# A decoder layer on one core: the self-attention output in seven block products, with new places for the mask and the first loads

## The chip, the cores and the metric

The kernel runs on one core of a Trainium2 chip. A core has five instruction queues that matter here: TensorE (PE, with PEld for its weight loads), VectorE (DVE), ScalarE (ACT), GpSimd (POOL) and SyncE (SP, which only issues transfers). Sixteen DMA engines move the data. The metric is device microseconds of the whole program, less is better. A measured time is the median of several runs; a profile is one further execution, with its own time.

## The reference, cut to what matters

The layer takes x of shape 8 x 256 x 1024 (eight batches, 256 tokens, 1024 features) and computes, all in float32:

```python
x = layernorm(x + self_attention(x))          # 32 heads of 32, 8 key/value heads, rotary, causal
x = layernorm(x + cross_attention(x, ctx))    # 32 heads of 128, 8 key/value heads, rotary, mask
x = layernorm(x + memory_ffn(x))

def self_attention(h):
    ...
    out = attn @ v                            # per head, put together to [8, 256, 1024]
    return out @ wo.T                         # wo 1024 x 1024
```

The change is about the last line, `out @ wo.T`, and about when some inputs are loaded. Per batch it is a product of 256 x 1024 by 1024 x 1024.

## The kernel before

Batches are counted from 0. Self-attention runs in 64 steps: step s belongs to batch b = s // 8 and to chunk c = s % 8, which is a group of four heads (128 features). The loop over s is at L508. It projects queries two steps ahead (`query(s + 2)`), makes scores one step ahead, and sums values for two steps at once: the even step of a pair only makes scores, the odd one does `weighted` in two halves. Between these the step does one thing from `others(s)` (L400). For c below 4 and b above 0 that is a quarter of the output projection of the batch before: `project_out(b - 1, c)` (L361) makes 128 tokens by 512 features in eight matmuls and adds it to the residual tile with one VectorE operation (L372). The quarters c = 0, 1 use the left half of the output weight, c = 2, 3 the right half. When both halves of a token tile are done, `moments` (L126 to L132) starts its norm; the reciprocal root is a GpSimd operation (L132). In chunks 4 to 7 `others` makes keys and values of the next batch, and `turn` (L383) transposes the normed tiles for cross-attention and stores them (x1T).

The output weight is loaded again for each batch. `load_out(b, 0)` issues four transfers of 512 KB at the end of chunk 6, `load_out(b, 1)` four more at the end of chunk 1 of the next batch (L353 to L358, tile `sa_wo`, four buffers). SP issues in program order, so a load that must wait for a buffer holds all loads behind it. Other weights go through nine buffers `w4` (L109).

From step 4 to 59 the same steps also make the keys and values of cross-attention, already by a seven-product scheme: `products` is a list of parts, four per step, taken by `one()` at fixed places. What these parts make is turned and stored by GpSimd: rotary adds `kx` (L725) with a store, and value stores (L835). The scheme needs sums of weight blocks. GpSimd makes them in "events" (`sum_event`, L483): event e issues the loads of its own tile `ws` (two buffers) and then does the four sums of event e - 1 (L417) and stores them to memory (L440, L466). As there are two buffers, the loads of event e wait until the stores of event e - 2, which were issued in event e - 1, have landed. The list `steps` says in which steps the events fall; one of a step's events comes right after `others`, the rest at the step's end (L567).

TensorE, GpSimd and SP run in exactly the order in which the program is written. VectorE and ScalarE are ordered by a planner.

The prologue (L493 to L506) loads the key weights of batch 0 and all of its input, makes both key projections, two queries, the scores of step 0 and the values of batch 0, and then loads the stored values back in a turned layout (`load_values`), which SP must wait for.

The passage to cross-attention starts at the end of step 61 with `xa_early`, which loads the first normed input (x1T), tables, keys, and last the mask; `mask_bias` turns the mask to a bias after the loop. In the wait listings SPq stands for SP's queue.

Of the kernel before, what the change touches and what calls it, by code (L numbers as in the profile page):

```python
# [8 lines left out]
F32 = mybir.dt.float32  # L9
# [3 lines left out]
ALU = mybir.AluOpType  # L13
# [7 lines left out]
P = 128  # L21
B, S, E = 8, 256, 1024
# [49 lines left out]
class Layer:  # L72
# [74 lines left out]
    def self_attention(self):  # L147
# [12 lines left out]
        def load_x(b):  # L160
            xTs[b] = ep.tile([P, KC, S], F32, name="xT", bufs=2)
            nc.sync.dma_start(out=xTs[b], in_=a["xT"][b])
# [10 lines left out]
        def load_kv(b, name):  # L173

            for i in range(2):
                src = a[name][:, :, i * P : (i + 1) * P] if name == "sa_wk" else a[name][:, 4 * i : 4 * i + 4, :]
                wkvs[b, name, i] = self.weights([P, *src.shape[1:]], src)

        load_kv(0, "sa_wk")
        load_x(0)  # L180
        nc.scalar.dma_start(out=rot, in_=a["sa_rot"])
        nc.scalar.dma_start(out=sin, in_=a["sa_sin"])
        nc.scalar.dma_start(out=cos, in_=a["sa_cos"])
# [1 line left out]
        def signed():  # L185

            ones = sp.tile([P, 1], F32, name="sa_ones")
            nc.gpsimd.memset(ones, 1.0)
            ps = self.mm()
            nc.tensor.matmul(ps[:, 0:1], lhsT=rot, rhs=ones, start=True, stop=True)  # L190
            sign = sp.tile([P, 1], F32, name="sign")
            nc.vector.tensor_copy(sign, ps[:, 0:1])
            nc.vector.tensor_scalar(sin, sin, sign, None, ALU.mult)
# [26 lines left out]
            nc.vector.tensor_tensor(turned, turned, sin, ALU.mult)  # L220
            nc.vector.tensor_tensor(dst, turned, dst, ALU.add)

        kTs, vs, v_d, qTs, ats, oTs = {}, {}, {}, {}, {}, {}

        def keys(b, i):
            if i == 0:
# [3 lines left out]
            rope(kTs[b][:, i, :], project(wkvs.pop((b, "sa_wk", i)), xTs[b]))  # L230

        def values(b, tt):
            if b and tt == 0:
                load_kv(b, "sa_wv")
            ps = self.mm()
            for k in range(KC):
                nc.tensor.matmul(
                    ps[:, :256], lhsT=xTs[b][:, k, tt * P : (tt + 1) * P],
                    rhs=wkvs[b, "sa_wv", k // 4][:, k % 4, :],
                    start=(k == 0), stop=(k == KC - 1),  # L240
                )
            rows = sp.tile([P, SA_KV * SA_D], F32, name="sa_vrow", bufs=2)
            nc.scalar.copy(rows, ps[:, :256])
            if tt == 0:
                v_d[b] = self.dram.tile([S, SA_KV * SA_D], F32, name=f"sa_v_{b}")
            nc.scalar.dma_start(out=v_d[b][tt * P : (tt + 1) * P, :], in_=rows)
# [69 lines left out]
        def weighted(s, rest):  # L316

            b, c = divmod(s, KC)
            at, v = ats[s // 2], vs[b, c // 4]
            if not rest:
                pos[s] = [p_sc.tile([P, 2, 512], F32, name="sc") for _ in range(2)]
            banks = [pos[s][i // 2][:, i % 2, :P] for i in range(4)]
            for k in range(3, BLOCKS) if rest else range(3):
                for i in range(max(k - 4, 0), 4):
                    rows = slice(32 * i, 32 * i + 32)
                    for j in range(4):
                        lo, block = (0, slice(2 * k, 2 * k + 2)) if k <= i else (  # L330
                            64, slice(2 * k + 1, 2 * k + 2) if k < 4 else slice(k + 4, k + 5)
                        )
                        nc.tensor.matmul(
                            banks[i][32 * j : 32 * j + 32, lo:], lhsT=v[rows, k, 32 * j : 32 * j + 32],
                            rhs=at[rows, j, block].rearrange("p x u q -> p (x u q)"),
                            start=(k == 0), stop=(k == 4 + i),
                        )
            if not rest:
                return
            del ats[s // 2], pos[s]  # L340
            oT = sp.tile([P, 2, S], F32, name="sa_oT", bufs=6)
            for i in range(4):
                nc.scalar.copy(
                    oT.rearrange("p u (t i q) -> p i t u q", t=2, i=4)[:, i],
                    banks[i].rearrange("p (t u q) -> p t u q", t=2, u=2),
                )
            for u in range(2):
                oTs[s - 1 + u] = oT[:, u, :]

        wos = {}  # L350
        norms = []

        def load_out(b, half):  # L353
            cols = slice(half * 512, (half + 1) * 512)
            wos[b, half] = []
            for c in range(0, KC, 2):
                w = sp.tile([P, 2, 512], F32, name="sa_wo", bufs=4)
                nc.sync.dma_start(out=w, in_=a["sa_wo"][:, c : c + 2, cols])  # L358
                wos[b, half].append(w)

        def project_out(b, i):  # L361
            half, tt = divmod(i, 2)
            t = 2 * b + tt
            cols = slice(half * 512, (half + 1) * 512)
            ps = self.mm()
            for c in range(KC):
                nc.tensor.matmul(  # L367
                    ps, lhsT=oTs[b * KC + c][:, tt * P : (tt + 1) * P], rhs=wos[b, half][c // 2][:, c % 2, :],
                    start=(c == 0), stop=(c == KC - 1),
                )  # L370
            x = self.res[t]
            nc.vector.tensor_tensor(x[:, cols], ps, x[:, cols], ALU.add)  # L372
            if half == 1:
                mv, rstd = self.moments(x, EPS)

                def norm():
                    nc.vector.tensor_scalar(x, x, mv[:, 0:1], rstd, ALU.subtract, ALU.mult)
                    self.x1[t] = self.dram.tile([P, E], F32, name=f"x1_{t}")
                    nc.scalar.dma_start(out=self.x1[t], in_=x)

                norms.append(norm)

        def turn(b, tt):  # L383

# [15 lines left out]
        def others(s):  # L400


            b, c = divmod(s, KC)
            parts = []
            if b and c < 4:
                parts.append(lambda: project_out(b - 1, c))
            elif c < 4 or 1 < b + 1 < B:
                parts.append([
                    lambda: values(b + 1, 0), lambda: values(b + 1, 1),
                    lambda: keys(b + 1, 0), lambda: keys(b + 1, 1),  # L410
                ][c % 4])
            if b and c in (5, 6):
                parts.append(lambda: turn(b - 1, c - 5))
            return parts
# [30 lines left out]
        def sums_of_outputs(g, u, half):  # L445
# [13 lines left out]
            def run():  # L459
# [6 lines left out]
                    nc.gpsimd.dma_start(out=self.wsums["xa_wo", g][i][:, u, cols], in_=t)  # L466
            return run


        sums = [lambda n=n, m=m, i=i: sums_of_inputs(n, m, i)  # L470
                for m in range(XA_KV // 2) for n in ("xa_wk", "xa_wv") for i in range(2)]
        sums += [lambda m=m, i=i: sums_of_inputs("xa_wq", m, i) for m in range(QP) for i in range(2)]
        sums += [lambda g=g, u=u, i=i: sums_of_outputs(g, u, i)
                 for g in range(XA_KV) for u in range(2) for i in range(2)]

        n = XA_KV * 2
        steps = [1 + e * 7 // 8 for e in range(n)]
        steps += [15 + e * (KV_END - 17) // (len(sums) - n) for e in range(len(sums) - n + 1)]  # L480
        made = []

# [7 lines left out]
        self.hp, self.raws = ep, 3  # L490
        products = [part for q in range(NQ) for m in range(XA_KV // 2) for part in self.xa_keys_values(q, m)]

        signed()  # L493
        keys(0, 0)
        load_query(0)
        load_kv(0, "sa_wv")
        keys(0, 1)
        load_query(1)
        load_x(1)
        load_query(2)  # L500
        query(0)
        values(0, 0)
        query(1)
        scores(0)
        values(0, 1)
        load_values(0, 0)  # L506
        last = SA_STEPS
        for s in range(last):  # L508
            b, c = divmod(s, KC)
# [44 lines left out]
            if s % 2:  # L554
                weighted(s, True)
                one()
                if s + 1 < last:
                    scores(s + 1)
            if c == 1:
                load_values(b, 1)  # L560
            elif c == 6:
                load_out(b, 0)
# [5 lines left out]
                event()  # L568
            if c == 7 and b + 1 < B:
                load_values(b + 1, 0)  # L570
            if b and c == 1:
                load_out(b - 1, 1)
            if b and c == 0 and b + 1 < B:
                load_x(b + 1)
            if first:
# [4 lines left out]
            if s == last - 3:  # L580
                early.close()
                self.xa_early()
                more = self.xa_query(1)
            if s == last - 1:
                psum.close()
                self.xa_psum()
        self.mask_bias()
# [17 lines left out]
    def xa_early(self):  # L605

        self.xp = self.hp = self.pool("xa_early", 1, side="right")
        self.raws = 2
        self.xb, self.kT, self.v, self.ats = {}, {}, {}, {}
        self.qT, self.atts, self.oT, self.wo, self.acc = {}, {}, {}, {}, {}  # L610
        self.queries = self.xa_query(0, eager=True)

        self.first_qTs = [self.qT_tile() for _ in range(2)]
        self.first_att = self.att_tile()
        self.bias = self.xp.tile([P, NB * 2, S], F32, name="bias")
        self.load_x1T(0)
        self.load_tables(0)
        self.load_keys(0)
        self.load_mask(0)

    def xa_psum(self):
        self.p_sc = self.pool("xa_sc", 2, space=PSUM)
# [973 lines left out]
```

## Time and profile before

| what | value |
|---|---|
| median of three runs | 3482.47 us (3478.1 to 3483.72) |
| the profiled execution | 3482.07 us |
| its span, first to last instruction | 3480.3 us |
| mean granted TensorE clock | 0.985 |
| busy PE / DVE / ACT / POOL | 97% / 61% / 35% / 30% |
| output projection of self-attention, TensorE (L367) | 224.8 us in 512 records |
| its adds, VectorE (L372) | 21.9 us, 32 of 686 ns |
| moved by DMA | 626.36 MB, mean 180 GB/s |

A line of the groups reads: line, engine, operation, out <- in, sizes, count, then busy us and mean ns of one, then idle us just before and what ended it. A line of a timeline reads: start, length, engine, line, operation, count, and in brackets the idle time before it with what ended it. A line of the waits reads: who waited for whom, us in total, times, longest us. "Releasers" are inferred from semaphores.

### The profile page before, as it was taken

How to read it: one execution, taken by the hardware profiler on the slowest of the kernel's cores; microseconds unless marked ns; L12 is line 12 of the kernel's file. 1: busy time of each engine (PE TensorE's matmuls, PEld its weight loads, DVE VectorE, ACT ScalarE, POOL GpSimd, SP SyncE). 2: the span in 40 equal slices, each digit the busy share in tenths (PEclk: the TensorE clock that was granted, in tenths of full speed). 3: DMA queues.
4: the chain of work that ended last, by engine and by line, in shares of the span. 5: the costliest groups of instructions: out<-in, count | busy, mean ns of one | idle time of the engine just before them, and what ended most of it. 6: DMA issues, size and time to landing. Idle time of an engine off the chain costs nothing.

```text
span 3480.3 us, 71081 instructions
## 1 busy us (share of the span) xinstructions
PE 3377.2 (97%) x27811; PEld 2448.8 (70%) x27811; DVE 2113.9 (61%) x6003; ACT 1202.3 (35%) x4030; POOL 1047.8 (30%) x1363
## 2 busy tenths in 40 slices
PE   7999999999999799999999999999999999999996
PEld 6777778787777567777667667676767766776763
DVE  4655565565566455665675566666665667566556
ACT  3434433343344333232223333223332333333224
POOL 3454655666655221121131112112111212121112
PEclk9999999999999899999999999999999999999998
DMA  7778788787877464444544444544444544444442
GB/s 234 231 245 271 262 267 266 264 279 246 285 270 240 167 192 150 136 138 132 167 149 146 125 127 137 163 143 149 135 131 131 161 146 146 133 127 135 130 148 97
DMA packets 269551, 626.36 MB, mean 180 GB/s; under 512 B 28961, under 2 KB 99761, under 8 KB 268193
## 3 DMA queue, kind: packets, MB, share of 16 engines
q1 hardware_dynamic: 194672, 441.00, 39.4%
q0 software_dynamic: 50032, 154.66, 14.0%
q10 hardware_dynamic: 24512, 26.15, 2.2%
q8 instruction: 221, 3.62, 0.4%
q14 instruction: 114, 0.93, 0.1%
HBM read 526.93 MB, written 94.77 MB: 179 GB/s over the span
## 4 chain that ended last, share of the span: by engine, by line
PE 61%; DVE 5%; POOL 1%; ACT 1%; issue 1%; DMA 1%; SPq 0%; POOLq 0%; DVEq 0%; ACTq 0%
PE mm L748 21%; PE mm L954 19%; PE mm L901 7%; PE sc L850 6%; PE mm L1232 2%; PE mm L367 2%; PE mm L1009 1%; PE mm L208 1%; PE mm L742 1%; POOL acc L983 1%; DVE res L983 0%; DVE t L723 0%; PE mm L1249 0%; DVE ln_st L126 0%; DVE xat L884 0%
## 5 line engine op out<-in xcount | busy, mean ns | idle before, releaser
L748 PE MATMUL mm<-x1T,w 128*128 128x256 f32 x3584 | 853.5, 382 | 15.3 <-DMA w<-xa_wq_sums 11.8
L748 PEld LDWEIGHTS mm<-x1T,w 128*128 128x128 f32 x3584 | 677.7, 191 | 201.6 <-issue 96.5
L954 PE MATMUL mm<-w,xoS 128*128 128x512 f32 x992 | 449.5, 596 | 0.0
L864 ACT ACTIVATE xatt<-xatt,nmax 128x256 f32<-128x256 f32 x512 | 257.2, 503 | 508.4 <-DVE nmax L859 499.0
L667 POOL DMA_DIRECT2D v<-v x256 | 151.4, 598 | 734.9 <-PE mm L901 616.9
L954 PE MATMUL mm<-w,xoT 128*128 128x512 f32 x744 | 338.1, 596 | 5.4 <-ACT xoT L909 4.1
L954 PEld LDWEIGHTS mm<-w,xoS 128*128 128x128 f32 x992 | 185.1, 190 | 193.3 <-issue 171.0
L208 PE MATMUL mm<-xT,w 128*128 128x256 f32 x1280 | 305.0, 395 | 9.3 <-DMA xT<-in_xT 9.3
L754 DVE TENSOR_TENSOR half<-mm,half 128x256 f32<-128x256 f32 x288 | 119.8, 416 | 291.7 <-PE mm L748 273.8
L208 PEld LDWEIGHTS mm<-xT,w 128*128 128x128 f32 x1280 | 246.4, 197 | 60.3 <-issue 25.0
L901 PEld LDWEIGHTS mm<-xat,v 32*128 32x128 f32 x8192 | 243.9, 187 | 53.4 <-issue 29.3
L920 POOL TENSOR_TENSOR xoS<-xoT 128x512 f32<-128x512 f32 x62 | 79.0, 1275 | 671.2 <-ACT xoT L909 670.9
L901 PE MATMUL mm<-xat,v 32*128 32x128 f32 x8192 | 269.9, 277 | 5.5 <-DVE acc L961 4.4
L289 ACT ACTIVATE att<-att,nmax 128x128 f32<-128x128 f32 (+1 forms) x512 | 225.5, 441 | 125.1 <-DVE nmax L284 124.9
L850 PE MATMUL sc<-kT,qT 128*128 128x256 f32 x1024 | 262.7, 380 | 0.0
L870 ACT ACTIVATE xatt<-xatt,rec 128x256 f32<-128x256 f32 x512 | 231.2, 499 | 88.1 <-DVE rec L868 87.7
L909 ACT COPY xoT<-mm 128x128 f32<-128x128 f32 x512 | 98.0, 275 | 470.0 <-PE mm L901 439.0
L754 DVE TENSOR_TENSOR raw<-mm,half 128x256 f32<-128x256 f32 x384 | 159.3, 415 | 159.2 <-PE mm L748 118.5
L417 POOL TENSOR_TENSOR ws<-ws 128x256 f32<-128x256 f32 x320 | 243.5, 761 | 27.8 <-DMA ws<-in_xa_wk 7.3
L954 PEld LDWEIGHTS mm<-w,xoT 128*128 128x128 f32 x744 | 138.7, 190 | 148.1 <-issue 127.3
L884 DVE STREAM_TRANSPOSE xat<-xatt 128x512 f32<-128x512 f32 x256 | 180.9, 707 | 74.7 <-ACT xatt L870 71.9
L367 PE MATMUL mm<-sa_wo,sa_oT 128*128 128x512 f32 x512 | 224.8, 592 | 0.0
(230 smaller groups left out, 4875.7 us busy)
## 6 DMA issues: line engine op xcount, KB each, us to landing
w<-xa_wq_sums SPq DMA_DIRECT2D x128, 512.0 KB, 3.7
w<-xa_wo_sums SPq DMA_DIRECT2D x124, 512.0 KB, 3.6
w<-in_xa_wo SPq DMA_DIRECT2D x97, 512.0 KB, 4.2
w<-in_sa_wq SPq DMA_DIRECT2D x64, 512.0 KB, 8.9
sa_wo<-in_sa_wo SPq DMA_DIRECT2D x64, 512.0 KB, 6.6
w<-in_xa_wq SPq DMA_DIRECT2D x64, 512.0 KB, 3.6
v<-v POOLq DMA_DIRECT2D x256, 128.0 KB
w<-xa_wk_sums SPq DMA_DIRECT2D x32, 512.0 KB, 8.6
```

Of the source, the lines that this page charges most:

```text
L208: nc.tensor.matmul(ps[:, :S], lhsT=lhs[:, k, :], rhs=xT[:, k, :], start=(k == 0), stop=(k == KC - 1),)
L289: nc.scalar.activation(att[:, jj, lo:hi], att[:, jj, lo:hi], AF.Exp, bias=nmax[:, i : i + 1], scale=-1.0, accum_out=sums[:, i : i + 1],)
L367: nc.tensor.matmul(ps, lhsT=oTs[b * KC + c][:, tt * P : (tt + 1) * P], rhs=wos[b, half][c // 2][:, c % 2, :], start=(c == 0), stop=(c == K ...
L417: nc.gpsimd.tensor_tensor(out, in0, in1, op)
L748: nc.tensor.matmul(ps[:, :S], lhsT=w[:, k, :], rhs=rhs[:, k, :], start=(k == 0), stop=(k == 3))
L754: nc.vector.tensor_tensor(out, in0, in1, ALU.add)
L850: nc.tensor.matmul(sc[:, qt, :], lhsT=qT[:, q0 : q0 + P], rhs=kT[:, b * S : (b + 1) * S], start=True, stop=True,)
L864: nc.scalar.activation(att[:, qt, :], att[:, qt, :], AF.Exp, bias=nmax[:, qt : qt + 1], scale=-1.0, accum_out=sums[:, qt : qt + 1],)
L870: nc.scalar.activation(att[:, qt, :], att[:, qt, :], AF.Identity, bias=0.0, scale=rec[:, qt : qt + 1])
L884: self.nc.vector.transpose(self.ats[M, b][:, :, u].rearrange("p c t j -> p t c j"), self.atts[H][b].rearrange("p t (c j) -> p t c j", j=32),)
L901: nc.tensor.matmul(banks[i][:, :P], lhsT=v[rows, c, :], rhs=at[rows, c, :], start=(c == 0), stop=(c == BLOCKS - 1),)
L954: nc.tensor.matmul(ps, lhsT=oT[lhs][:, u, off + p * P : off + (p + 1) * P], rhs=w[:, u, :], start=(u == 0), stop=(u == 1),)
```

## The change

For batches 1 to 6 the output projection is made by seven block products. The attention output of a batch, 256 x 1024, is split into 2 x 2 blocks of 128 x 512 (A11 to A22), the weight into 2 x 2 blocks of 512 x 512. Four sums of A blocks (S1 to S4) and four of weight blocks (T1 to T4) make seven products of four matmuls take the place of eight (four quarters of eight matmuls). Each product is added to up to four blocks of the residual: 14 additions per batch in place of 4. Chunk 0 makes P1 and P2, chunk 1 P6 and P5, chunk 2 P3 and P4, chunk 3 P7.

The sums of A are made by GpSimd: S1 and S2 at the end of chunk 7, S4 and S3 at the end of chunk 1, in each case behind the step's events. The sums of the weight are made once, by eight further events among the first, and stored; each is loaded again per batch. Each of the seven products loads its own 1 MB of weights (two transfers), at the ends of chunks 6, 0, 1 and 2.

In the prologue the first key weight and the first input are loaded in halves by turns, queries and scores of step 0 come before the values, the value weights of batch 1 are loaded there, and the values are loaded back in steps 0 and 1. The mask is loaded at the end of step 63.

```diff
-        load_kv(0, "sa_wk")
-        load_x(0)
+        for k in range(0, KC, 4):
+            nc.sync.dma_start(out=first_k[:, k : k + 4, :], in_=a["sa_wk"][:, k : k + 4, :P])
+            nc.sync.dma_start(out=xTs[0][:, k : k + 4, :], in_=a["xT"][0][:, k : k + 4, :])
...
         def load_out(b, half):
+            if 0 < b < B - 1:
+                return load_seven(b, ("P1", "P2")) if half == 0 else None
...
+        PARTS = {
+            "P1": ("A11", (0, 0)), "P2": ("A12", (1, 0)), "P3": ("S4", (1, 1)), "P4": ("A22", "T4"),
+            "P5": ("S1", "T1"), "P6": ("S2", "T2"), "P7": ("S3", "T3"),
+        }
...
+        def sum_heads(b, name):
+            out = sp.tile([P, 4, P], F32, name="sa_S", bufs=2)
+            pieces = [out[:, 0:2, :], out[:, 2:4, :]]
...
+            for o, u, v in zip(pieces, x, y):
+                nc.gpsimd.tensor_tensor(o, u, v, op)
...
+        def seventh(b, n):
+            ps = self.mm()
...
+            for k in range(4):
+                nc.tensor.matmul(
+                    ps, lhsT=left[k // 2][:, k % 2, :], rhs=w[k // 2][:, k % 2, :],
+                    start=(k == 0), stop=(k == 3),
+                )
+            return ps
...
+        def out_by_seven(b, c):
+            if c == 0:
+                add_to(b, seventh(b, "P1"), (0, 0), (0, 1), (1, 0), (1, 1))
+                add_to(b, seventh(b, "P2"), (0, 0))
+            elif c == 1:
+                add_to(b, seventh(b, "P6"), (0, 1), (1, 0), (1, 1))
+                add_to(b, seventh(b, "P5"), (0, 1), (1, 1))
+            elif c == 2:
+                add_to(b, seventh(b, "P3"), (0, 1))
+                norm_later(2 * b)
+                add_to(b, seventh(b, "P4"), (1, 0))
+            else:
+                add_to(b, seventh(b, "P7"), (1, 0), (1, 1))
+                norm_later(2 * b + 1)
...
+        for e in range(8):
+            sums.insert(3 * e + 2, lambda e=e: sums_of_sa(e // 2, e % 2))
...
-        n = XA_KV * 2
-        steps = [1 + e * 7 // 8 for e in range(n)]
+        n = XA_KV * 2 + 8
+        steps = [1 + (e - e // 3) * 7 // 8 for e in range(n)]
...
+        load_query(0)
+        load_query(1)
+        load_kv(0, "sa_wv")
+        nc.sync.dma_start(out=wkvs[0, "sa_wk", 1], in_=a["sa_wk"][:, :, P:])
+        load_query(2)
+        load_x(1)
         signed()
         keys(0, 0)
...
+        load_kv(1, "sa_wv")
+        query(0)
+        scores(0)
+        query(1)
+        values(0, 0)
+        values(0, 1)
+        keys(0, 1)
...
+            if s < 2:
+                load_values(0, s)
+            elif c == 1:
                 load_values(b, 1)
...
             while events:
                 event()
...
+            if c == 7 and 0 < b < B - 1:
+                sum_heads(b, "S1")
+                sum_heads(b, "S2")
+            if c == 0 and 0 < b - 1 < B - 1:
+                load_seven(b - 1, ("P6", "P5"))
+            if c == 2 and 0 < b - 1 < B - 1:
+                load_seven(b - 1, ("P7",))
             if b and c == 1:
                 load_out(b - 1, 1)
+                if 0 < b - 1 < B - 1:
+                    load_seven(b - 1, ("P3", "P4"))
+                    sum_heads(b - 1, "S4")
+                    sum_heads(b - 1, "S3")
...
             if s == last - 1:
+                self.load_mask(0)
                 psum.close()
...
         self.load_keys(0)
-        self.load_mask(0)
```

`sums_of_sa` is `sums_of_outputs` (L445) with the four blocks of `sa_wo`: two loads, four subtractions and four stores of 128 KB per event.

## The prediction

> **What bounds the kernel now.** [...]I read the page's totals first, then TensorE's timeline through self-attention for its idle gaps, then the waits of SP and GpSimd, then GpSimd's timeline around the output projection.
>
> ```profile
> PE 3377.2 (97%) x27811; PEld 2448.8 (70%) x27811; DVE 2113.9 (61%) x6003; ACT 1202.3 (35%) x4030; POOL 1047.8 (30%) x1363
> ...
> L367 PE MATMUL mm<-sa_wo,sa_oT 128*128 128x512 f32 x512 | 224.8, 592 | 0.0
> ```
>
> TensorE is busy for 97% of the span, so only two things pay: fewer matmuls, or one of its few gaps closed. Equally, whatever holds TensorE back costs in full. L367, the projection that is rewritten, never waits. Its 512 records are 256 matmuls (two records for one f32 matmul); the chain has a product of eight (x16) at 6.87 us, 0.859 us each.
>
> ```profile
> 12.75 13.63 PE L208 MATMUL mm<-xT,w 128*128 128x256 f32 x48 [9.35 <-DMA xT<-in_xT]
> ...
> 49.19 5.58 PE L237 MATMUL mm<-w,xT 128*128 128x256 f32 x16 [6.87 <-DMA w<-in_sa_wv]
> ...
> 1198.11 14.89 PE L748 MATMUL mm<-x1T,w 128*128 128x256 f32 x56 [11.79 <-DMA w<-xa_wq_sums]
> ```
>
> These are the gaps (in brackets) that the moved loads aim at: 9.35 us for the first input, 6.87 us for a value weight, 11.79 us at the passage to cross-attention. After a gap the engine is slow: the 5.58 us are the same sixteen records that take 3.62 us elsewhere.
>
> ```profile
> 653.16 1.43 POOL L440 DMA_DIRECT2D xa_wq_sums<-ws  x2 [0.30 <-POOL ws L417]
> ...
> 659.19 1.27 POOL L725 TENSOR_TENSOR kx<-kx,t 128x512 f32<-128x512 f32 x1 [2.42 <-DVE t L724]
> 660.75 0.56 POOL L830 DMA_DIRECT2D kT<-kx  x1 [0.30 <-DMA xa_wq_sums<-ws]
> 661.31 1.44 POOL L429 DMA_DIRECT2D ws<-in_xa_wq  x2
> 662.77 3.15 POOL L417 TENSOR_TENSOR ws<-ws 128x256 f32<-128x256 f32 x4
> 666.23 1.43 POOL L440 DMA_DIRECT2D xa_wq_sums<-ws  x2 [0.30 <-POOL ws L417]
> ```
>
> This is GpSimd in step 33 (batch 3's projection, part c = 1). It looks idle at 30%, but it works through "weight sum" events in order, and each waits until the last one's stores have landed. From the norm of one batch to the projection of the next it runs at its own pace, some 12 us per event at 1.5 events per 18 us step.
>
> **The change, part by part.** The sum is against the profiled execution: span 3480.3 us, its run 3482.07 us (1.8 us outside the span); the median of the runs is 3482.47 us, 0.4 us above that run.
>
> *Products.* Six batches go from 32 to 28 matmuls: 24 x 0.859 = **-20.6 us**. All of it falls in step c = 3, which keeps one product of four.
>
> *Start.* Before the first product SP now loads 1.5 MB, not 2, in two halves. Before, 2 MB landed at 12.7 us at about 0.25 MB per us on this queue, so the halves come at about 7 and 10.5 us. Then, from TensorE's durations: half a cold key product 7 to 10, the rest to 13.7, query to 17.1, about 2 us for its rotary chain, scores to 20.1, one query, two values, one key (3.45 each) to 33.9, scores, query, values to 41.7. The weighted sum of step 1 started at 54.7; its softmax, with 8 to 11 us behind scores that end at 34.8, allows about 43.3. The second batch's value weights are now issued ahead of the loads that wait for the stored values (SP sat until 42.5 us there), so the 6.87 us gap goes. **-11 us**; between -13 and -7.
>
> *Mask.* SP waited for the completion of an x1T store before the mask, with four 512 KB output weights and the awaited sums behind it:
>
> ```profile
> SPq L109 <- DMA x1T<-w: 9.9, 1, 9.9
> ```
>
> The wait lists of the built program give that same wait to the first of the four output weights once the mask is gone. So the sums leave at about 1187.8 instead of 1188.2, with 2.5 MB ahead and with them instead of 3: a sixth of 9.8 us. **-2 us**, not -11.8; the bounds are 0 and -4. In its new place the mask follows the sums; its bias (0.69 us on VectorE) lies under seven products.
>
> *Sums of the output weight.* Eight more events, each 1.44 + 3.16 us and four stores (2.2 us in the row of the cross-attention output sums): 8 x 7 = 56 us of GpSimd between steps 2 and 15, with perhaps 4 us of landing each. GpSimd waited some 90 us on other engines between 97 and 303 us, so most is covered; uncovered, it would delay the weight sums that SP fetches, which have about 30 us to spare. The last event ends late: behind the rotary add at 302.6 there are now two events and S1, S2, so S2 is ready at about 326 where TensorE wants it at 323.2, and T2's load is as late. **+3 us** (0 to +12).
>
> *Adds.* 14 instead of 4 per batch on VectorE at 686 ns (line L372): 60 x 0.69 = 41 us. They stand mostly behind the softmax, where VectorE is idle (12 to 15 us busy in an 18 us step), but P1's PSUM bank is held through four adds and the third product after it wants that bank about 0.7 us early: six times, less what falls before a wait that is there anyway, **+3 us** (0 to +12).
>
> *Loads.* 7 MB per batch instead of 4, and 8 MB for the sums: 26 MB, all behind SP's new waits at c = 0, 1 and 2. P6 and P5 have 10 us between P2's end and their use and need about 7; P3 and P4 have 15. I take 0; where the DMA engines are already full (0.99 to 1.04 busy at 370 to 400 GB/s just after c = 1) it could be +15.
>
> *Head sums.* S1 and S2 have about 3 us to spare or more in later batches. **S4 has not.** P3 needs it, in step c = 2, and in GpSimd's order it stands behind both events of step c = 1 and the rotary add or value store of that step's last product. The list: when that row ends in the trace, plus 0.76 us for S4's first half (the event's tensor operation), less the start of the projection at c = 2 (TensorE's timeline):
>
> batch 1: 354.1 + 0.8 - 349.2 = 5.6; batch 2: 511.2 + 0.8 - 504.9 = 7.0; batch 3: 667.7 + 0.8 - 661.1 = 7.3; batch 4: 816.5 + 0.8 - 811.3 = 5.9; batch 5: 971.1 + 0.8 - 969.2 = 2.6; batch 6: 1117.6 + 0.8 - 1118.8, nothing.
>
> That is 28.4 us. S1 and S2 put 3 us more ahead of it, hidden in waits for stores except in batches 3 and 4: +4. A gap of 2.3 us at 365.7 us falls into batch 1's wait: -2.3. In order behind S4 stand the norms' rstd and the next event, which TensorE's delay covers. A stall in one batch doesn't shorten the next, because GpSimd waits for the norms in steps c = 2 and 3 (9 to 10 us in the rows) and starts again from there.
>
> **Two rules against rows.** First, the stores. The Trainium skill (DMA: Bandwidth & Descriptors, Anatomy of one DMA) puts a GpSimd transfer at 2.0 us plus bytes / 436e3, 2.6 us for 256 KB. In batch 2 the store issued at 494.9 frees its buffer at 503.4, 8.5 us later; batch 4 has 9.8. By the rule batches 2, 4 and 5 would wait 1.1, 2.9 and 0, and the sum of S4's waits would be 17, not 28. I take the rows. Second, the clock. The skill (TensorE: Matmul & The Clock Gate, Part 1) says that after an idle window of about 3.4 us the array runs at half speed for as long, 1.7 us lost, and nothing after shorter gaps. The row after 6.87 us loses 1.96 us, and one after only 2.7 us (the query at 344.8: 4.59 for 3.72 us) still 0.9. So four long stalls and a short one add 4 x 1.9 + 0.9 = **+8.5 us**, by the rule 6.8.
>
> S4 in all: 28.4 + 4 - 2.3 + 8.5 = **+38.6 us**.
>
> Sum: -20.6 - 11 - 2 + 3 + 3 + 38.6 = **+11 us**. Span 3491, median about 3493; I say 3492.
>
> **The rivals.** *S4 comes in time* (faster): stores land quicker, or VectorE and GpSimd gain while TensorE is slower, and the last wait at c = 2 remains TensorE's own. Then -20.6 - 11 - 2 + 6 = -28, 3455 us. For it: GpSimd's 30%, and S4's tensor work of 1.5 us. Against: the order is fixed and the rows are full. *Half of it*, by the skill's landing time and clock: S4 costs 17 + 7, the whole is -4, or -10 if the sums and adds are hidden too: 3472 to 3479. *Transfers become the bound* (slower still): if a third of 26 MB at 400 GB/s (65 us) comes on top, 3515 us. For it: the full DMA rows after c = 1. Against: TensorE waits for no sa_wo there today. That the mask move frees nothing is in the sum.
>
> **How the numbers follow.** The limit of what can be told apart is 0.2%, 7 us. S4 late as listed: 0.50, own range 3476 to 3508 (0.36 slower, 0.12 within, 0.02 faster). S4 in time: 0.23, faster. Half of it: 0.15 (0.07 faster, 0.08 within). Transfers: 0.12, slower. Together faster 0.32, within 0.20, slower 0.48. The range 3456 to 3514 leaves out about 0.1 below and 0.07 above.
>
> **What would show it.** In the changed profile TensorE's timeline has waits of 5 to 10 us for the head sums on GpSimd before the product of four at c = 2 in batches 1 to 5, and half-speed matmuls behind them; the weighted sum of step 1 starts near 43 us; L367's successors have 168 + 64 matmuls; the wait for xa_wq_sums is still near 10 us. I am wrong if that wait at c = 2 is missing, or if TensorE waits for sa_wo transfers instead.

## The result, and the profile after

The changed kernel took 3519.76 us (median of 4 runs, 3513.57 to 3520.12) against 3481.03 us for the kernel before on the same chip: a ratio of 1.011, 95% interval 1.0095 to 1.0125. It is 38 us slower. The prediction was 3492 us, with a range up to 3514: the sign was right, the size was short by 28 us.

The profiled execution has a span of 3518.0 us (3480.3 before). First the page's totals, with the busy time of each engine:

```profile
PE 3373.3 (96%) x27763; PEld 2443.6 (69%) x27763; DVE 2142.0 (61%) x6063; ACT 1202.0 (34%) x4030; POOL 1130.1 (32%) x1491
```

TensorE is busy 3.9 us less, VectorE 28 us more, GpSimd 82 us more. The 24 products did go (20.6 us), so 16.7 us came back in TensorE's own row. Of these, 12.6 us are slow matmuls in five rows that are shown below. The groups of the rewritten projection, with busy time, mean ns of one record, and the idle time ahead of them:

```profile
L434 PE MATMUL mm<-sa_wo,sa_S 128*128 128x512 f32 x192 | 98.0, 664 | 35.0 <-POOL sa_S L425 35.0
L434 PE MATMUL mm<-sa_wo,sa_oT 128*128 128x512 f32 x144 | 63.8, 592 | 0.0
L376 PE MATMUL mm<-sa_wo,sa_oT 128*128 128x512 f32 x128 | 56.1, 592 | 0.0
```

These are 168 + 64 matmuls. Those that read a head sum (sa_S) waited 35.0 us, where the old projection never waited, and need 664 instead of 592 ns each. TensorE's timeline shows where, and also the start, the early steps and the passage to cross-attention:

```profile
5.81 3.40 PE L214 MATMUL mm<-xT,w 128*128 128x256 f32 x8 [1.44 <-DMA xT<-in_xT]
...
43.85 0.40 PE L339 MATMUL sc<-at,sa_v 32*32 32x128 f32 x2 [0.54 <-DVE at L306]
...
186.28 3.62 PE L873 MATMUL mm<-w,ctxT 128*128 128x128 f32 x16 [3.64 <-DMA w<-xa_wv_sums]
...
229.15 1.99 PE L273 MATMUL sc<-sa_kT,sa_qT 32*128 32x128 f32 x16 [5.61 <-ACT sa_oT L349]
...
353.62 0.80 PE L273 MATMUL sc<-sa_kT,sa_qT 32*128 32x128 f32 x4 [7.63 <-DVE nmax L290]
...
369.02 6.13 PE L434 MATMUL mm<-sa_wo,sa_S 128*128 128x512 f32 x8 [7.03 <-POOL sa_S L425]
...
528.16 6.77 PE L434 MATMUL mm<-sa_wo,sa_S 128*128 128x512 f32 x8 [7.77 <-POOL sa_S L425]
...
691.00 5.57 PE L434 MATMUL mm<-sa_wo,sa_S 128*128 128x512 f32 x8 [6.97 <-POOL sa_S L425]
...
846.74 6.20 PE L434 MATMUL mm<-sa_wo,sa_S 128*128 128x512 f32 x8 [8.38 <-POOL sa_S L425]
...
1011.18 5.91 PE L434 MATMUL mm<-sa_wo,sa_S 128*128 128x512 f32 x8 [4.37 <-POOL sa_S L425]
...
1234.32 5.92 PE L879 MATMUL mm<-x1T,w 128*128 128x256 f32 x19 [11.02 <-DMA w<-xa_wq_sums]
```

The five rows of L434 are P3 in batches 1 to 5: 34.5 us of waiting for S4, and 30.6 us for what takes 5 x 3.60 = 18.0 elsewhere, so 12.6 us more. That is the clock: over these five stretches the granted TensorE clock was 0.60, 0.54, 0.66, 0.59 and 0.62. The three rows at 186, 229 and 353 us are gaps that the kernel before has not, or only as 2.1 us, and no product of seven stands in them. Compared with the kernel before, the first projection starts 8.3 us early (148.8 for 157.2 us) but batch 1's starts 5.3 us late (311.2 for 305.9): 13.6 us are lost before the first of the seven products.

GpSimd's timeline ahead of the first long wait:

```profile
361.91 1.42 POOL L521 DMA_DIRECT2D ws<-in_xa_wq  x2 [2.62 <-DMA xa_wq_sums<-ws]
363.35 3.14 POOL L509 TENSOR_TENSOR ws<-ws 128x256 f32<-128x256 f32 x4
366.79 1.42 POOL L532 DMA_DIRECT2D xa_wq_sums<-ws  x2 [0.30 <-POOL ws L509]
368.01 1.63 POOL L425 TENSOR_TENSOR sa_S<-sa_oT,sa_S 128x256 f32<-128x256 f32 x2
```

S4 (L425) follows right behind an event; its first half is ready at about 369, when P3 starts.

### The profile page after: what moved, and what is told of

Read it like the earlier page. It is cut to its first block, busy times and chain, and to the rows that moved or that the text cites. A ratio compares the mean times of both kernels' runs of the same rounds, so it can differ in the third digit from the quotient of the medians.

```text
span 3518.0 us, 71282 instructions
## 1 busy us (share of the span) xinstructions
PE 3373.3 (96%) x27763; PEld 2443.6 (69%) x27763; DVE 2142.0 (61%) x6063; ACT 1202.0 (34%) x4030; POOL 1130.1 (32%) x1491
## 4 chain that ended last, share of the span: by engine, by line
PE 62%; DVE 5%; POOL 1%; DMA 1%; issue 1%; ACT 1%; SPq 0%; POOLq 0%; DVEq 0%; ACTq 0%
PE mm L879 21%; PE mm L1085 19%; PE mm L1032 7%; PE sc L981 6%; PE mm L1363 2%; PE mm L214 1%; PE mm L434 1%; PE mm L873 1%; PE mm L1140 1%; PE mm L376 1%; POOL acc L1114 1%; PE sc L339 0%; DVE res L1114 0%; DVE t L854 0%; PE mm L1380 0%
## 5 line engine op out<-in xcount | busy, mean ns | idle before, releaser
L1032 PEld LDWEIGHTS mm<-xat,v 32*128 32x128 f32 x8192 | 245.0, 188 | 53.4 <-issue 29.3
L509 POOL TENSOR_TENSOR ws<-ws 128x256 f32<-128x256 f32 x352 | 263.8, 749 | 28.1 <-DMA ws<-in_xa_wk 5.6
L873 PEld LDWEIGHTS mm<-w,ctxT 128*128 128x128 f32 x1792 | 209.2, 193 | 21.6 <-issue 13.2
```

The source lines that it names most:

```text
L509: nc.gpsimd.tensor_tensor(out, in0, in1, op)
L873: nc.tensor.matmul(ps[:, t * P : (t + 1) * P], lhsT=rhs[:, k, t * P : (t + 1) * P], rhs=w[:, k, :], start=(k == 0), stop=(k == 3),)
L1032: nc.tensor.matmul(banks[i][:, :P], lhsT=v[rows, c, :], rhs=at[rows, c, :], start=(c == 0), stop=(c == BLOCKS - 1),)
```

## The experiments

Differences below are ratios, each against the kernel before on the same chip, times 3481 us: that kernel's own median lay between 3477.6 and 3481.7 us in the four sessions, which is as much as some effects. One per mille is 3.5 us. A single profiled execution lay up to 9 us below the median of its kernel's runs, so profiles are used for places and gaps, ratios for sizes. Line numbers of a kernel's groups shift by a few with its edit.

**S4 ahead of the events.** After the products of step c = 1 (P5 has to be done, since S4 takes S1's buffer), before the next event:

```diff
+            if c == 1 and 0 < b - 1 < B - 1:
+                sum_heads(b - 1, "S4")
+                sum_heads(b - 1, "S3")
             event()
...
-                    sum_heads(b - 1, "S4")
-                    sum_heads(b - 1, "S3")
```

> S4 and S3 are issued on GpSimd ahead of the weight-sum events of step c = 1 instead of behind them; nothing else changes. Theory A (S4 stands behind those events, 34.5 us of gaps before P3 in batches 1 to 5 and 12.6 us of slow matmuls behind them): the gaps before P3 fall under 3 us, P3's sixteen records return to about 3.6 us, and of the 47 us some 35 to 45 come back, 3475 to 3485 us; a little is lost since the events now start after P5. Rival T (the 26 MB of added loads, or the adds on VectorE, hold TensorE back): P3 then waits for its weights or a bank in place of S4, and the time stays at 3505 to 3520 us.

3485.71 us, ratio 1.0023 (1.0014 to 1.0032): +8 us instead of +38. The move gives back 0.87% with an interval of about 0.17, 30 us plus or minus 6. The five waits are gone; the same product of batch 1 (eight records, not sixteen as the expectation says):

```profile
357.56 3.60 PE L434 MATMUL mm<-sa_wo,sa_S 128*128 128x512 f32 x8
```

**No sums of the output weight.** The eight added events left out, and T1 to T4 replaced by plain blocks of the weight. Like some of the kernels below, this one leaves out part of the layer's arithmetic and only times what is left:

```diff
-                        nc.sync.dma_start(out=w, in_=sa_sums[int(src[1]) - 1][:, c : c + 2, :])
+                        nc.sync.dma_start(out=w, in_=a["sa_wo"][:, c : c + 2, 512 * (int(src[1]) % 2) : 512 * (int(src[1]) % 2) + 512])
...
-        for e in range(8):
-            sums.insert(3 * e + 2, lambda e=e: sums_of_sa(e // 2, e % 2))
```

> The eight added weight-sum events are left out; T1 to T4 are replaced by plain blocks of the output weight (as many bytes loaded), so batches one to six get a wrong output projection. S4 stays late. Theory B (the eight events on GpSimd between steps 2 and 15 delay the norms' reciprocal roots, the cross-attention sums and the context loads behind SP): 15 to 20 us come back, 3500 to 3505 us, the gaps at about 186, 229 and 353 us go, and the offset against the kernel before is near -10 us at batch 1's first projection step instead of +5. Rival (the loss before batch 1 comes from the new order of the first loads): at most 4 us come back, 3516 us or more.

3502.29 us, ratio 1.0072 (1.0055 to 1.0088): 13 us (plus or minus 8) came back. Batch 1's first projection starts at 296.5 us, 9.4 ahead of the kernel before, as the theory said, and the gaps at 186 and 229 are gone. The third one is not: 4.6 us before a softmax are left of 7.6. S4 still costs 34 us of waits there.

**Both edits.** The two diffs above together.

> Both edits at once: S4 ahead of the events, and no sums of the output weight (plain blocks loaded in place of T1 to T4, output of batches one to six wrong). If the two causes are separate and are all that goes against the change, the rest of the sum is left: products -20.6, start -11, mask -2, adds +3 on 3481, so 3450 us; 3450 to 3460. Rival T (loads or adds cost 10 us or more): 3462 us or more.

3467.77 us, ratio 0.9965 (0.9957 to 0.9973): -12 us. The sums cost 20 us (plus or minus 4) once S4 is out of the way. But it is 18 us above the rest of the sum: a third cost exists, which the theory of S4 and the sums does not have. In its timeline these three gaps name a transfer or a softmax and are longer than with the new start alone, the run after this one (2.8 us in place of 6.4, and none above 2 us in place of the others):

```profile
334.21 0.80 PE L273 MATMUL sc<-sa_kT,sa_qT 32*128 32x128 f32 x4 [6.38 <-DVE nmax L290]
...
623.45 2.40 PE L838 MATMUL mm<-ident,w 128*128 128x128 f32 x8 [3.72 <-DMA w<-in_xa_table,pos_u]
...
956.91 3.25 PE L878 MATMUL mm<-ctxT,w 128*128 128x256 f32 x8 [2.21 <-DMA w<-xa_wk_sums]
```

The first is VectorE held by a late load, one row earlier in its own timeline; the softmax stands behind it:

```profile
331.82 1.23 DVE L767 TENSOR_TENSOR ctxT<-ctxT 128x1024 f32<-128x1024 f32 x1 [8.16 <-DMA ctxT<-in_ctxT]
```

None of these is a load of the output weight. All are loads beside it or behind it. One more gap, 4.0 us at 358 us, ends when VectorE has made an addition (L443) that frees the product's bank.

**The new start alone,** on the kernel before: the hunks of the change that split the first loads, issue them and the first products in the new order, fetch batch 1's value weights early, and put the first two value loads into the steps.

```diff
-            if b and tt == 0:
+            if b > 1 and tt == 0:
...
-            if c == 1:
+            if s < 2:
+                load_values(0, s)
+            elif c == 1:
```

> The kernel before with only the new order of the first loads and products. By the sum -11 us: 3470 us (3468 to 3474), and the weighted sum of step 1 starts at about 43.5 us. Rival (the head start is taken back later by the work that GpSimd and SP pace between steps 2 and 16): within 4 us of the kernel before, 3477 to 3483 us.

3469.50 us, ratio 0.9979 (0.9969 to 0.9990): -7 us, between the two expectations. The profile has the first projection 9.5 us early and keeps that to batch 1.

**Fewer adds, fewer loads.** Two kernels made from the one with both edits ask which of the two is the third cost. The first adds each product to one block only:

```diff
-            for tt, half in parts:
+            for tt, half in parts[:1]:
```

> The kernel with both edits (S4 ahead of the events, no sums of the output weight; 3467.8 us) with each of the seven products added to one block only: 7 instead of 14 adds per batch on VectorE, the same products and loads; batches one to six get a wrong output projection. That kernel is 15 to 20 us above its sum of 3450. Theory V (the adds hold VectorE and the PSUM banks): the 4 us gap before the context product at 358 us goes and 10 us or more come back, 3458 us or less. Theory L (the loads behind SP's new waits): at most 4 us, 3464 us or more.

The second loads four parts of the weight per batch and uses three of them twice:

```diff
-            w = sevens.pop((b, n))
+            w = sevens[b, {"P6": "P1", "P5": "P2", "P7": "P3"}.get(n, n)]
...
-            if c == 0 and 0 < b - 1 < B - 1:
-                load_seven(b - 1, ("P6", "P5"))
-            if c == 2 and 0 < b - 1 < B - 1:
-                load_seven(b - 1, ("P7",))
```

> The kernel with both edits (3467.8 us) with four instead of seven parts of the output weight loaded per batch, at the two places of the kernel before: P6, P5 and P7 read the tiles of P1, P2 and P3, so SP's waits at c = 0 and c = 2 go, and 18 MB of loads; output wrong as there. Theory L: 10 us or more come back, 3458 us or less, the gaps on the context load at 334 us, on the table at 623 us and on the key sums at 957 us shrink to those of the kernel with the new start alone. Theory V: at most 4 us, 3464 us or more.

Without seven of the fourteen adds: ratio 0.9963 (0.9949 to 0.9977), 1 us from the kernel with all of them, within its error of 6, and 3.1 us of the gap at 358 us stay, which theory V expected to go. Without the 18 MB: 3453.16 us, ratio 0.9920 (0.9903 to 0.9937), 16 us (plus or minus 7) better. So it is the loads. In that profile the gap before the softmax is 2.4 us and those at 623 and 957 us are gone, though one of 6.4 us for a key sum stands at 878 us, where both edits have 2.9.

This kernel leaves out the bytes and also SP's waits for buffers. A third one keeps every transfer in SP's order and cuts its bytes, here and in the same way for the blocks in place of T1 to T4:

```diff
-                            out=w, in_=a["sa_wo"][:, 4 * k + c : 4 * k + c + 2, half * 512 : half * 512 + 512]
+                            out=w[:, :, :64], in_=a["sa_wo"][:, 4 * k + c : 4 * k + c + 2, half * 512 : half * 512 + 64]
...
-                    ps, lhsT=left[k // 2][:, k % 2, :], rhs=w[k // 2][:, k % 2, :],
+                    ps, lhsT=left[k // 2][:, k % 2, :], rhs=w[k // 2][:, k % 2, :64].rearrange("p (a n) -> p a n", a=1).to_broadcast([P, 8, 64]),
```

> The kernel with both edits (S4 ahead, no sums; 3467.8 us) in which every load of the output weight for the seven products brings only 64 of 512 columns, which the matmuls read eight times over: the same number of transfers at the same places of SP's order with the same waits, and an eighth of the bytes (5 of 42 MB); output of batches one to six wrong. With 18 MB and the waits at c = 0 and c = 2 gone that kernel had 3453. Theory bytes (the transfers fill the DMA engines and the context, table and sum loads land late): 3456 us or less. Theory order (SP stands at the buffers of the output weight with the other loads behind it): 3462 us or more.

3457.94 us, ratio 0.9940 (0.9923 to 0.9957): 9 us (plus or minus 7) better, between the two expectations. SP's waits at the buffers of the output weight from 280 to 1100 us stay as long as they were, first with both edits, then here:

```profile
SPq L401 <- PE mm L434: 211.3, 45, 20.6
```

```profile
SPq L401 <- PE mm L434: 235.1, 48, 21.6
```

The other loads come sooner all the same: the issue table has a query weight (w<-in_sa_wq) land 6.2 us after its issue instead of 9.4 (medians), and a key sum 5.4 instead of 8.2. VectorE's waits for the context load are, in this order, with the start alone, with both edits, without the 18 MB and with an eighth of the bytes:

```profile
DVE ctxT L645 <- DMA ctxT<-in_ctxT: 4.6, 1, 4.6
```

```profile
DVE ctxT L767 <- DMA ctxT<-in_ctxT: 10.3, 2, 8.2
```

```profile
DVE ctxT L763 <- DMA ctxT<-in_ctxT: 4.2, 1, 4.2
```

```profile
DVE ctxT L767 <- DMA ctxT<-in_ctxT: 2.1, 2, 1.1
```

At this one place the traces tell bytes from order. With both edits SP issued the four context loads at 318.6 us, 1.7 us earlier than without the 18 MB (320.3), so waits in SP's order did not hold them back. But issuing them took 7.6 us instead of 2.7, they landed 11.5 us after their issue instead of 9.5, and from 290 to 340 us the DMA engines were busy for 0.92 at 304 GB/s instead of 0.73 at 242.

For the cost as a whole there is no such division. The kernel with an eighth of the bytes moves 37 MB less, twice what was added. If the time goes with the bytes, 18 MB would be worth 9 x 18 / 37 = 4 us, an estimate with an error nearly as large. Nor do the added loads show in the two medians: with the start alone they are 9.6 and 8.3 us. So the added loads cost 16 us (plus or minus 7), and how these divide between their bytes and their places in SP's order is not shown.

**The eight events on the kernel before.** The same events, at the same places, results unused (the function that makes them is the change's, with its own DRAM tiles):

```diff
+        for e in range(8):
+            sums.insert(3 * e + 2, lambda e=e: sums_of_sa(e // 2, e % 2))
...
-        n = XA_KV * 2
-        steps = [1 + e * 7 // 8 for e in range(n)]
+        n = XA_KV * 2 + 8
+        steps = [1 + (e - e // 3) * 7 // 8 for e in range(n)]
```

> The kernel before with the eight weight-sum events added in the first steps, their results not used; nothing else. Theory B, by the 17 us that came back when they were left out: 12 to 18 us slower than the kernel before. Rival (the events cost only where the seven products and the earlier start need GpSimd, SP and VectorE at the same time): under 5 us.

3500.00 us, ratio 1.0053 (1.0036 to 1.0069): +18 us by themselves, without an early start or a seven-product form beside them. TensorE's new gaps, and GpSimd's timeline in one of them:

```profile
192.71 2.88 PE L769 MATMUL mm<-w,ctxT 128*128 128x128 f32 x16 [2.79 <-DMA w<-xa_wv_sums]
...
236.01 1.99 PE L267 MATMUL sc<-sa_kT,sa_qT 32*128 32x128 f32 x16 [6.06 <-ACT sa_oT L343]
...
356.76 0.49 PE L267 MATMUL sc<-sa_kT,sa_qT 32*128 32x128 f32 x4 [4.35 <-DVE nmax L284]
...
385.54 1.55 PE L735 MATMUL mm<-ident,w 128*128 128x128 f32 x6 [5.98 <-DVE raw L781]
```

```profile
215.57 2.19 POOL L491 DMA_DIRECT2D sa_wo_sums<-ws  x4
217.78 0.60 POOL L132 TENSOR_TENSOR ln_rstd<-ln_ve,neghalf 128x1 f32<-128x1 f32 x1
225.80 1.49 POOL L429 DMA_DIRECT2D ws<-in_xa_wv  x2 [7.42 <-DMA sa_wo_sums<-ws]
227.31 3.14 POOL L417 TENSOR_TENSOR ws<-ws 128x256 f32<-128x256 f32 x4
230.75 1.43 POOL L440 DMA_DIRECT2D xa_wv_sums<-ws  x2 [0.30 <-POOL ws L417]
231.94 1.74 POOL L862 DMA_DIRECT2D v<-raw  x2
233.47 0.80 POOL L132 TENSOR_TENSOR ln_rstd<-ln_ve,neghalf 128x1 f32<-128x1 f32 x1
```

After four stores of an added event (L491) GpSimd waits 7.42 us until they have landed and the buffer can be filled again; behind that wait stand the next event, a value store and the norm's reciprocal root (L132 at 233.47). VectorE stands at the norm for 7.4 us, until 234.3 us. The two lists of GpSimd's waits from 20 to 320 us show what was used up. Before:

```profile
POOL kx L725 <- DVE t L724: 53.4, 6, 15.5
...
POOL ln_rstd L132 <- DVE ln_ve L130: 21.7, 2, 13.1
POOL v L835 <- DVE raw L754: 16.8, 4, 7.8
```

With the events:

```profile
POOL ws L429 <- DMA sa_wo_sums<-ws: 39.8, 7, 7.5
...
POOL v L862 <- DVE raw L781: 5.2, 1, 5.2
...
POOL kx L752 <- DVE t L751: 1.6, 1, 1.6
```

The 92 us in which GpSimd waited for VectorE's work (53.4 + 21.7 + 16.8) were its slack. The events take 8 x 6.8 us of instructions and 39.8 us of landing, 94 us. Of the 92 us, 6.8 are left (5.2 + 1.6), and GpSimd is late for the root and for SP's sums.

**What carries the cost of the events.** First the norm issued later on VectorE, at the end of its step, here on the kernel before with the events:

```diff
-            while norms:
-                norms.pop(0)()
+            due, norms[:] = norms[:], []
             for part in others(s):
...
+            for norm in due:
+                norm()
             if s + 3 < last:
                 load_query(s + 3)
```

> The kernel before with the eight added events (18 to 20 us slower than before) and with each norm issued on VectorE at the end of its step instead of ahead of the step's projection, so that VectorE doesn't stand at the reciprocal root that GpSimd makes behind an event. Theory R (the events cost through that root): the waits for ln_rstd of 8.5, 7.4 and 10.0 us on VectorE shrink below 3 us, TensorE's gaps of 6.1 us at 236 and 6.0 us at 386 go, and 8 to 14 us come back, 3486 to 3492 us. Rival (the sums and context loads that SP waits for): at most 4 us, 3496 us or more.

Ratio 1.0042 (1.0024 to 1.0060), 3498.6 us; 4 us, not told from none. VectorE's waits for the root were 11.0, 9.1 and 10.1 us, no shorter than the 8.5, 7.4 and 10.0 with the events alone: the test did not take away what it should, since GpSimd itself is late. The same edit in the changed kernel with S4 ahead:

> The changed kernel with S4 ahead of the events (3485.7 us) and the late norm; complete and meant to run. Theory R: 8 to 14 us come back, 3472 to 3478 us. Rival: 3482 us or more.

Ratio 1.0003 (0.9992 to 1.0013), 3481.16 us: 7 us better than without it, level with the kernel before; between the expectations.

The root taken off GpSimd for the norms of self-attention, where a plain addition on VectorE stands in its place and the root is left out. The control has the same edit without the events:

```diff
-        nc.gpsimd.tensor_tensor(rstd, ve, self.neghalf, ALU.pow)
+        nc.vector.tensor_scalar(rstd, ve, 1.0, None, ALU.add)
```

> The kernel before with the eight added events (0.53% or 18 to 20 us slower), and the norm's scale in self-attention made on VectorE from variance plus constants in place of the reciprocal root on GpSimd; the root is left out there, so the output is wrong. Theory R (the events cost because the root waits behind them on GpSimd and VectorE stands there): 10 us or more come back, 3490 us or less, and the gaps at 236 and 386 us go. Theory W (late cross-attention sums and context loads on SP): at most 5 us, 3495 us or more, with gaps at 193 and 357 us at least as long.

> The control: the kernel before with the same plain scale in place of the root, no added events; the root left out. Its one wait for the root of 6.3 us at 364 us, with a gap of 2.3 us on TensorE, goes: 0 to 4 us faster, 3477 to 3482 us, whichever theory holds. If it gains as much as the kernel with the events does, theory R falls.

With the events 1.0033 (1.0022 to 1.0044), without them 0.9992 (0.9982 to 1.0002). The difference of the two is 0.41%, 14 us, where it was 18: the root carries some 4 us (plus or minus 8) of it. The median of 3489.53 us lies in theory R's range only because the kernel before was 1.9 us faster on that chip; by the ratio 7 us came back, not 10 or more. R, that the root is the main way, is not borne out, though the error does not exclude it. The gaps at 236 and 386 us go, as R said. But the one behind the softmax stays (3.4 us, at 347 us), and a new one of 5.5 us stands at 374 us, at a table that GpSimd itself gathers. In the changed kernel with S4 ahead:

> The changed kernel with S4 ahead of the events (3485.7 us) and the plain scale on VectorE in place of the root; root left out. Theory R: 12 to 18 us come back, 3468 to 3474 us, near the kernel without the sums (3467.8). Theory W: at most 6 us, 3480 us or more.

Ratio 0.9994 (0.9979 to 1.0009), 10 us (plus or minus 6) better than with the root, of which the control explains 3; between the expectations again.

The stores left out:

```diff
-                for i, t in enumerate((b11, b22, b12, b21)):
-                    nc.gpsimd.dma_start(out=spare[i][:, k, cols], in_=t)
```

> The kernel before with the eight added events without their four stores each; loads and tensor operations stay, and the sums are not kept. Theory S (GpSimd's 39.8 us of waits for stores that have to land before the buffer is filled again are the price): 10 us or more come back, 3490 us or less. Rival (the 56 us of issue and tensor work are the price): 3495 us or more.

3481.77 us, ratio 1.0011 (1.0002 to 1.0021): 15 of the 18 us go with the stores. Issue of the loads and tensor work, 37 us of GpSimd, cost only 4. The waits for VectorE are partly back: 24.2 us for kx, 9.0 for the values and 8.1 for the root, 41 us in all. So the price of the events is mainly their stores: 17.5 us to issue and 39.8 us to wait for. The 4 MB that the stores move went with them; that these bytes cost little is likely (37 MB were worth 9 us above) but was not tested alone. How it is passed on is spread: a part by the root, the rest by sums, tables and context loads that come late. It was not separated further.

**Two versions meant to run.** With S4 ahead, the events moved to steps 15 to 20 and the seven products from batch 2 on:

```diff
-            sums.insert(3 * e + 2, lambda e=e: sums_of_sa(e // 2, e % 2))
+            sums.append(lambda e=e: sums_of_sa(e // 2, e % 2))
...
-        n = XA_KV * 2 + 8
+        n = XA_KV * 2
...
-            if 0 < b < B - 1:
+            if 1 < b < B - 1:
```

> A version meant to run: S4 ahead of the events, the eight events moved behind the cross-attention key and value sums (steps 15 to 20, where GpSimd has 1.7 events per step from then on), and the seven products from batch two on, so 20 products are saved instead of 24. Theory B: the 17 us of the early events come back and 3.4 us of products are lost, 3470 to 3474 us, which is no better than the new start alone (3469.5). Rival (denser events later are as dear as early ones): 3480 us or more.

3511.67 us, ratio 1.0094 (1.0077 to 1.0110), a clear miss. The events are as dear there or dearer. A likely reason, not tested, is that from then on GpSimd has 72 events in 43 steps instead of 64. VectorE's waits after 300 us have a row that was 9.7 us in the kernel before:

```profile
DVE res L467 <- POOL ln_rstd L132: 55.0, 12, 12.4
```

And last, the start with the later norm of above and the mask behind the sums, without the seven products:

```diff
-        self.load_mask(0)
...
             if s == last - 1:
+                self.load_mask(0)
                 psum.close()
```

> A version meant to run: the kernel before with the new start, the mask behind the sums, and the late norm, without the seven products. Start -8 to -11 us, mask -1 to -2, and the late norm takes away what is left of VectorE's wait of 6.3 us for ln_rstd at 364 us (a gap of 2.3 us in TensorE): 3466 to 3470 us. If the late norm delays the turned rows or a residual: 3472 us or more.

3471.83 us, ratio 0.9975 (0.9965 to 0.9985): 9 us faster than the kernel before, not told apart from the start alone. These two are the only complete versions that beat both kernels. The wait for xa_wq_sums is 10.8 us there, 13.0 with the start alone, 11.8 before.

## Why the prediction was right or wrong

| term | predicted, us | measured, us | by |
|---|---|---|---|
| products | -20.6 | -20.5 ± 7, with adds and mask | without the 18 MB (0.9920) against the start alone (0.9979); 168 + 64 matmuls, 592 ns where no head sum is late |
| start | -11 | -7 ± 4 | the start alone |
| mask | -2 | about -1 | the wait for xa_wq_sums, 11.0 for 11.8 us; by times not told from none |
| sums | +3 | +20 ± 4 (+18 ± 6) | both edits; on the kernel before |
| adds | +3 | +1 ± 6 | seven of the ten new ones left out |
| loads | 0 | +16 ± 7 | four parts instead of seven |
| S4 with its clock | +38.6 | +30 ± 6 | S4 ahead |
| together | +11 | +38 | the terms, with the products at -20.6, make +38 |

S4, sums, loads, products and start are the steps of one chain of kernels, from the changed one to the one before, so what was measured adds up by construction. The step with the products checks the account: it is worth what was said, within its error of 7 us.

That the change would lose was right for the reason given, S4. The size was wrong by two other terms: sums and loads cost 33 us more than was said, S4 cost 9 us less and the start gave 4 us less.

*S4*: right in place, cause and batch. The listed waits were 5.6, 7.0, 7.3, 5.9, 2.6 and 0 us; the profile has 7.0, 7.8, 7.0, 8.4, 4.4 and none. In gaps and slow matmuls it is 47.1 us, more than said; in time only 30 came back. Part of the rest is other late work that TensorE meets with S4 ahead: a wait of 6.0 us at 376 us for a bank that VectorE holds and one of 3.6 us at 640 us for a table are new, and those at 223 us (6.8, ScalarE's copy) and 350 us (8.3, a softmax) are 1.2 and 0.7 us longer than in the changed kernel. Here the gaps were longer than what their removal gave.

*Start*: the weighted sum of step 1 came at 43.85 us (43.3 said). The later loss of 3 to 4 us is within the error.

*Adds*: within their range. VectorE had more room than was read: in the kernel before it is busy for 7 to 13 us, not 12 to 15, in the eight steps that project the outputs of batches 2 and 3.

*Sums*: the first step that failed. The term was +3 us and measured +20 ± 4. It said that GpSimd's 90 us of waits cover most of the events. The 90 us are there, but so was the bill: with the stores' landing put at "perhaps 4 us" it was already 56 + 32 = 88, and in the trace it is 54 us of instructions and 40 us of landing, 94. Cover that is used up is no cover: with 7 us of these waits left the events cost 18 us, without the stores, with 41 us left, 4 us. Through which of the operations behind GpSimd the time is lost stays open. The upper bound of +12 was too low too.

*Loads*: the second step that failed. The term was 0 and measured +16 ± 7. It looked only for TensorE waiting for the output weight, and that is still right: no such wait exists in any of these profiles. What it left out are the other loads: the context load landed later, VectorE and then TensorE stood for it. How the 16 us divide between bytes and order stays open. The bound of +15 had the price, but tied it to full DMA engines just after c = 1. The rival of transfers comes nearest to the result with 3515 us, and that is luck: it has S4 as in the sum, and all the rest in the transfers, with nothing more for the sums.

*The two rules.* For stores, the row was right and the figure of the Trainium skill (DMA: Bandwidth & Descriptors, Anatomy of one DMA) was not one to use here: four stores of 128 KB, 2.3 us each by that fit (an estimate), hold their buffer until 8 us after the last issue (217.8 to 225.8). With the rule's landing time S4 would have been 17 us; its gaps were 34.5. For the clock, five gaps of 4.4 to 8.4 us lost 2.0 to 3.2 us each, 12.6 in all. The prediction's 1.7 us by the skill (TensorE: Matmul & The Clock Gate, Part 1) is an estimate, half of the page's window of about 3.4 us, which the page calls free-running. Five times that makes 8.5, and my 1.9 was low as well.

*The range* ended at 3514, 6 us below the result. It took in one of the two unknown costs, sums or loads, at its bound, not both.

## What to carry to other kernels

An engine that works in program order and is busy for 30% may have no room: add up the waits that it has in the stretch concerned, compare them with the new work including the time for its stores to land, and count what stands behind it as late when the two are near each other. A load that is itself in time can still cost time: ask for every added transfer which other load lands later, not only who waits for it. And when a small operation feeds the bound engine, place it ahead of the background work in the program order of its engine: two calls moved were worth 30 us here.

## What was not expected of the hardware

Small stores set the price: the stores of eight events, four of 128 KB each, carry 15 us (plus or minus 7) of 18, while the loads and tensor work of the same events, 37 us of GpSimd, cost 4. And 84 loads of the output weight with an eighth of the bytes, at the same places of the queue, brought the median landing of other loads from 9.4 to 6.2 us and from 8.2 to 5.4 us.
